# Scaling the weights of the later projections two pairs ahead, with the first scalings tied to the program's order

## The chip, the core and the metric

The kernel runs on one core of a Trainium2 chip. A core has five engines that work side by side, each through its own instructions in order: TensorE (PE in the profile, its weight loads PEld), VectorE (DVE), ScalarE (ACT), GpSimd (POOL) and SyncE (SP), which here only issues DMA transfers. They meet through semaphores. The metric is the device time of one execution in microseconds (us); less is better. All data is float32.

## The reference

Two layers work on x of shape 4 x 512 x 128 x 64 (batch b, time t, and f x h, together d = 8192). The part that matters is the beginning of layer 0:

```
xn = layernorm(x.reshape(b, t, d), ln_attn_g, ln_attn_b)
k = xn @ Wk
v = xn @ Wv
r = sigmoid(xn @ Wr)          # Wk, Wv, Wr: 8192 x 64
s_t = decay * s_(t-1) + k_t * v_t     # scan over time
x = x + (r * states) @ Wo
```

After it layer 0 has a convolution over frequency (with a norm and a gelu), a depthwise convolution over time (with two norms) and a feed-forward block from 64 to 256 and back. Layer 1 takes a moving average over time, filters the rest in the Fourier domain with 128 modes, and adds both.

## The kernel before

The 8192 features lie on partitions in 64 chunks of 128. Nearly all loops of layer 0 run over 32 *pairs* of chunks (`NPR`), with the 512 times along the free axis. For each batch there are these stages, written as generators:

- `project` (J): k, v, r and one more product, summed in PSUM over all pairs,
- `scan` (Z): the norm applied afterwards to the summed products, and the scan over time,
- `attend_and_convolve` (A), `convolve_time` (C), `open_feed` (O) and `feed_forward` (F).

The first norm is not applied to x. Its scale `ln_attn_g` is multiplied into the weights, and its mean and variance are applied in `scan`. So `project` loads, for each pair, the weights and the transposed x (`load_x`, line 295), multiplies the weights by the scale (`scale_weights`, line 358: two VectorE instructions of 128 x 192 for a pair, one for each chunk j), and multiplies (line 409: two products of 128 x 512 for each chunk in the program, each of which is two in the trace). Besides, x is loaded a second time with time on partitions (line 333), and VectorE takes its statistics (`statistics`, line 341).

For batches 2 and 3, which this text calls the later projections (`b > 1`), the weights come two pairs at a time (`weights`, line 351, 512 KB, issued on SP at every even pair for the two pairs after next). They lie in a ring of two buffers (`wx`). The scan uses the same ring for its own scratch (lines 474 to 487), and for b of 2 and 3 `feed_forward` uses it for line 758. Activations (`xp`) have a ring of three.

**Order.** TensorE's order is the program's own (`manual_schedule`). `in_turn` takes two stages of different batches at a time and draws from the two generators by fixed shares. Batch 2 is projected while batch 0 is in its feed-forward block, batch 3 while batch 1 is. At the end of each projection its scan runs between the last steps of the same feed-forward block. At its beginning the ends of `attend_and_convolve` and `convolve_time` are in TensorE's order: `finish` (line 264 sums, line 269 copies) and `moments` (lines 275 to 278, with a power of -1/2 on GpSimd, lines 233 and 234).

The orders of VectorE, ScalarE, GpSimd and SP are made by a planner when the program is built: it sets instructions by their readiness in its own model, and an instruction whose inputs it takes to be early may move far ahead of its place in the program. `tc.keep_in_program_order(i)` forbids that in one respect: i stays behind the instruction that the program wrote just before it for the same engine. It is no wait. If that earlier instruction has itself been moved ahead, i may move ahead with it.

In the feed-forward block, which runs beside the later projections, `widen` multiplies (line 732), ScalarE applies the gelu (line 737), `narrow` multiplies back (line 745) and ends with line 758 on VectorE, and `store` transposes its result on TensorE (line 764). VectorE also makes the next inputs there (lines 691, 692, 703) and, in the projections' first parts, time convolutions for the next batch (lines 613, 616, 625).

In the scan, line 470 multiplies k and v into place, lines 474 to 489 end in the state, lines 483 to 491 in `rst`, which line 496 multiplies.

## Time and profile before

| what | value |
| --- | --- |
| median of 3 runs | 3748.59 us |
| the runs | 3748.67, 3748.59, 3736.15 us |
| profiled execution | 3734.79 us |
| its span, first to last instruction | 3733.0 us |
| mean granted TensorE clock | 0.981 |
| TensorE busy | 3521.2 us, 94% |
| VectorE busy | 2671.9 us, 72% |
| ScalarE busy | 1778.0 us, 48% |
| later projections | about 795 to 1140 us and 1465 to 1806 us |
| their scans | about 1140 to 1200 us and 1806 to 1870 us |

In the profile's lines a group is named by line, engine, operation and output <- input, with the numbers of buffers left out. In a timeline a line holds the start, the duration, the instruction and how many of it follow each other; a bracket gives the idle time of the engine before it and what ended that. `DMA` in a bracket is a transfer, `issue` is time in which the engine waited for nothing that the profile shows.

### The profile page before, as it was taken

To read this page: it belongs to the slowest core of one execution; us is meant where nothing else is said; L and a number is where in the kernel's file an instruction comes from. 1 tells how busy PE (TensorE), PEld (TensorE's weight loads), DVE (VectorE), ACT (ScalarE), POOL (GpSimd) and SP (SyncE) were. 2 spreads that over 40 slices of the span, in tenths; PEclk is the share of its full clock that TensorE was granted. 3 is DMA by queue.
4 is the path that set the end of the run, shared out by engine and by line. 5 is a ranking of instruction groups with operands and counts; after the bars stand their busy time and mean duration, and the time that the engine had idled before them with its cause. 6 is when DMAs were issued, how large, how long until landed. Compare 5 with 4: busy or idle time off the path is not lost. (4 is left out here: it accounts for less than half of the span.)

```text
span 3733.0 us, 53000 instructions
## 1 busy us (share of the span) xinstructions
PE 3521.2 (94%) x20041; PEld 1360.6 (36%) x20041; DVE 2671.9 (72%) x3498; ACT 1778.0 (48%) x2331; POOL 447.3 (12%) x654
## 2 busy tenths in 40 slices
PE   9999999999998999999989989999989999989998
PEld 4433322234333223433322233333323843328533
DVE  4455569976776896676789699946658277792677
ACT  0012346655656565565656578868854200152100
POOL 0000012210101221001122122100000000001000
PEclk9999999999999999999999999999999999999999
DMA  9867657787874687788578677645569478894687
GB/s 314 279 211 242 227 177 262 260 276 265 290 262 168 235 280 271 266 292 278 182 238 286 213 247 267 234 149 196 198 203 287 150 240 290 290 297 164 213 294 260
DMA packets 427223, 910.29 MB, mean 244 GB/s; under 512 B 32728, under 2 KB 83160, under 8 KB 422872
## 3 DMA queue, kind: packets, MB, share of 16 engines
q1 hardware_dynamic: 353136, 636.92, 52.5%
q0 software_dynamic: 71680, 268.46, 19.7%
q8 instruction: 160, 2.62, 0.3%
q10 hardware_dynamic: 2152, 1.51, 0.1%
q14 instruction: 95, 0.78, 0.1%
HBM read 638.26 MB, written 268.50 MB: 243 GB/s over the span
## 5 line engine op out<-in xcount | busy, mean ns | idle before, releaser
L745 PE MATMUL p<-mid,w_sb 64*64 64x512 f32 x2048 | 554.5, 599 | 20.3 <-DVE wx L758 20.3
L745 PE MATMUL pb<-mid,w_sb 64*64 64x512 f32 x2048 | 536.2, 598 | 0.0
L737 ACT ACTIVATE mid<-c,fb_sb 128x1024 f32<-128x1024 f32 x256 | 284.3, 1111 | 97.2 <-PE c L732 94.8
L737 ACT ACTIVATE mid<-m,fb_sb 128x1024 f32<-128x1024 f32 x256 | 284.6, 1112 | 93.5 <-PE m L732 92.1
L732 PE MATMUL c<-x,w_sb 64*64 64x512 f32 x2016 | 281.2, 611 | 13.2 <-ACT mid L737 6.9
L732 PE MATMUL m<-x,w_sb 64*64 64x512 f32 x2016 | 283.0, 612 | 6.7 <-ACT ob L777 4.9
L745 PEld LDWEIGHTS p<-mid,w_sb 64*64 64x64 f32 x2048 | 155.5, 135 | 294.9 <-issue 262.0
L409 PE MATMUL a<-xp,wx 128*128 128x512 f32 x512 | 242.6, 617 | 9.1 <-DVE wx L358 8.6
L1043 ACT COPY two<-a 128x512 f32<-128x512 f32 x64 | 37.5, 585 | 428.9 <-PE a L1038 428.9
L1066 PE MATMUL b<-xin,avg_sb 128*128 128x512 f32 x512 | 230.8, 593 | 3.3 <-DVE xin L1072 3.3
L1072 DVE TENSOR_TENSOR xin<-b,pm 128x512 f32<-128x512 f32 x256 | 159.1, 683 | 100.2 <-PE b L1069 85.3
L570 ACT ACTIVATE sq<-x 128x1024 f32<-128x1024 f32 x128 | 135.1, 1055 | 181.4 <-DVE x L567 181.3
L625 DVE SCALAR_TENSOR_TENSOR to<-kd,vec,to 128x510 f32<-128x510 f32 (+1 forms) x272 | 197.1, 744 | 9.8 <-ACT to L621 8.7
L700 ACT ACTIVATE kd<-kd,vec 128x512 f32<-128x512 f32 x256 | 192.8, 803 | 3.1 <-DVE kd L692 3.1
L252 PE MATMUL st<-x,ones 128*32 128x512 f32 x512 | 176.8, 603 | 13.1 <-DVE x L567 13.1
L925 DVE COPY xf<-b 128x256 f32<-128x256 f32 x128 | 54.4, 425 | 178.3 <-PE b L1012 169.4
L625 DVE SCALAR_TENSOR_TENSOR z<-x,vec,z 128x511 f32<-128x511 f32 x240 | 175.9, 745 | 5.3 <-ACT z L621 3.0
L531 DVE TENSOR_TENSOR x<-a,xp 128x1024 f32<-128x1024 f32 x128 | 156.1, 1220 | 30.6 <-PE a L529 28.4
L703 DVE TENSOR_TENSOR x<-kd,kx 128x1024 f32<-128x1024 f32 x126 | 154.1, 1223 | 32.8 <-ACT kd L700 32.7
L529 PE MATMUL a<-rst,wo_sb 64*128 64x512 f32 x512 | 147.0, 648 | 27.1 <-DVE x L531 25.1
L758 DVE SCALAR_TENSOR_TENSOR x4t<-p,fb_sb,x 128x512 f32<-128x512 f32 x64 | 47.9, 748 | 172.0 <-PE pb L745 169.6
L692 DVE TENSOR_TENSOR kd<-kd,rm 128x1024 f32<-128x1024 f32 x128 | 155.7, 1220 | 7.8 <-ACT rm L286 6.3
(269 smaller groups left out, 6755.1 us busy)
## 6 DMA issues: line engine op xcount, KB each, us to landing
xp<-in_xt SPq DMA_DIRECT2D x256, 512.0 KB
kh<-to SPq DMA_DIRECT2D x156, 512.0 KB
x<-x POOLq DMA_DIRECT2D x128, 512.0 KB, 4.6
kx<-x SPq DMA_DIRECT2D x128, 512.0 KB
x<-ob POOLq DMA_DIRECT2D x64, 1024.0 KB, 8.0
xin<-x SPq DMA_DIRECT2D x64, 1024.0 KB
out<-xin POOLq DMA_DIRECT2D x64, 1024.0 KB, 6.6
x<-x SPq DMA_DIRECT2D x96, 512.0 KB
```

What stands on the lines that cost most here:

```text
L252: nc.tensor.matmul(st[32 * q : 32 * q + 32, :], lhsT=ones, rhs=src[:, j, :], start=first, stop=last,)
L409: nc.tensor.matmul(pa[:, k, :], lhsT=wq[:, j, k * P : (k + 1) * P], rhs=xp[:, j, :], start=first and j == 0, stop=last and j == 1,)
L531: nc.vector.tensor_tensor(x1, at, xp, ALU.add)
L625: tap = nc.vector.scalar_tensor_tensor(to[:, j, k:], xr[:, j, : SL - k], vec[:, w, c], to[:, j, k:], ALU.mult, ALU.add)
L692: nc.vector.tensor_tensor(d, d, pair_of(mb), ALU.subtract)
L700: tc.keep_in_program_order(nc.scalar.activation(d[:, j, :], d[:, j, :], AF.Identity, bias=vec[:, B4, c], scale=vec[:, G4, c]))
L703: nc.vector.tensor_tensor(x3, d, x2, ALU.add)
L732: nc.tensor.matmul(pm[halves[j], h, :], lhsT=w1_sb[halves[h], q * H : (q + 1) * H], rhs=x3[halves[h], j, :], start=True, stop=True,)
L737: nc.scalar.activation(mid, pm, AF.Gelu_apprx_tanh, bias=fb1_sb[:, q : q + 1])
L745: nc.tensor.matmul(sums2[i][j][halves[h], :], lhsT=w2_sb[halves[j], q, :], rhs=mid[halves[j], h, :], start=q == 0, stop=q == 3,)
L1066: nc.tensor.matmul(po[j], lhsT=avg_sb[:, j, :], rhs=xin[:, j, :], start=True, stop=False)
L1072: nc.vector.tensor_tensor(by_n(xin[:, j, :]), by_n(po[j]), by_c(pm[j % 2][:, j // 2, :]), ALU.add)
```

## The change

In the later projections:

- the scalings of the first *two* pairs are written ahead of the loop, and both are tied to the program's order (before: the first pair's only, and not tied),
- in the loop the scaling of pair i + 2 is written behind the products of pair i, where before the scaling of pair i + 1 was written ahead of the products of pair i. All of them are tied, as before.

Batches 0 and 1 are as they were, and so is the number of instructions.

```diff
         if b > 1:
             weights(0)
-            scale_weights(0, ws[0])
+            for k in range(2):
+                scale_weights(k, ws[k], True)
             xps[0] = load_x(b, 0)
...
             if b < 2:
                 scale_weights(i, wq)
-            elif not last:
-                scale_weights(i + 1, ws[i + 1], True)
             for j in range(2):
                 for k in range(2):
                     nc.tensor.matmul(
                         pa[:, k, :], lhsT=wq[:, j, k * P : (k + 1) * P], rhs=xp[:, j, :],
                         start=first and j == 0, stop=last and j == 1,
                     )
+                if b > 1 and j == 1 and i + 2 < NPR:
+                    scale_weights(i + 2, ws[i + 2], True)
                 yield 1.0
```

In the built program TensorE's order is the same before and after. VectorE's changes as follows. Before, the six scalings of the first three half buffers (pairs 0 to 2) stand in the scan of the batch before, some 300 instructions ahead of their products; after, they stand behind line 278 of the moments that the program writes just before the projection. In the loop the two scalings of a slot stand ahead of its two statistics instead of behind them, and in parts of the projection a scaling stands one slot earlier. On SP two loads change places with a neighbour, one in each later projection.

## The prediction

> **What bounds the kernel now.** I read the page's head first, then the chain that ended last, the waits of TensorE, and the timelines of TensorE and VectorE at every wait that has to do with line 358. The head:

> ```profile
> span 3733.0 us, 53000 instructions
> PE 3521.2 (94%) x20041; PEld 1360.6 (36%) x20041; DVE 2671.9 (72%) x3498; ACT 1778.0 (48%) x2331; POOL 447.3 (12%) x654
> L409 PE MATMUL a<-xp,wx 128*128 128x512 f32 x512 | 242.6, 617 | 9.1 <-DVE wx L358 8.6
> ```

> TensorE is the bound, busy for 94%, and its order is written out by hand. A time is gained or lost only where TensorE stands still or runs at half clock. Its waits, with total, count and longest:

> ```profile
> PE c L764 <- DVE x4t L758: 15.9, 9, 4.7
> PE a L409 <- DVE wx L358: 8.6, 2, 4.3
> PE m L764 <- DVE x4t L758: 8.1, 7, 4.3
> ```

> The second line is the scaling itself coming late, once in each later projection. TensorE's timeline, then VectorE's, around the first:

> ```profile
> 1054.95 3.78 PE L409 MATMUL a<-xp,wx 128*128 128x512 f32 x4 [4.29 <-DVE wx L358]
> ```

> ```profile
> 1052.26 1.22 DVE L616 TENSOR_TENSOR x<-x,rm 128x1024 f32<-128x1024 f32 x1
> 1053.39 1.28 DVE L341 BATCH_NORM_STATS2 stt<-x 128x6 f32<-128x512 f32 x2
> 1054.59 0.53 DVE L358 TENSOR_SCALAR wx<-wx,vec 128x192 f32<-128x192 f32 x2
> ```

> Here two pairs' products follow each other without a feed-forward block between them. The second pair's scaling stands behind VectorE work that took until 1054.6. The same wait, also 4.29 us, ends at 1720.83 in the last projection. The 4.3 and 4.7 us of line 764 are less plain. They lie in the scan of batch 2, at 1150 to 1178; VectorE first:

> ```profile
> 1156.41 0.55 DVE L358 TENSOR_SCALAR wx<-wx,vec 128x192 f32<-128x192 f32 x2 [3.31 <-DMA wx<-in_wkvr]
> 1156.87 0.75 DVE L758 SCALAR_TENSOR_TENSOR x4t<-p,fb_sb,x 128x512 f32<-128x512 f32 x1
> ...
> 1174.15 0.55 DVE L358 TENSOR_SCALAR wx<-wx,vec 128x192 f32<-128x192 f32 x2 [3.42 <-DMA wx<-in_wkvr]
> 1174.61 0.74 DVE L758 SCALAR_TENSOR_TENSOR x4t<-p,fb_sb,x 128x512 f32<-128x512 f32 x1
> ```

> ```profile
> 1157.77 1.09 PE L764 MATMUL m<-ident,x4t 128*128 128x128 f32 x4 [4.30 <-DVE x4t L758]
> ...
> 1175.50 1.09 PE L764 MATMUL c<-ident,x4t 128*128 128x128 f32 x4 [4.71 <-DVE x4t L758]
> ...
> 1184.29 0.64 PE L496 MATMUL a<-rst,qo 64*64 64x512 f32 x1
> ```

> These scalings belong to batch 3, whose products start at 1465. The planner has floated them 300 us ahead, where VectorE stops for weights just asked for (issues at 1146.15 and 1170.75) and line 758 stands behind it.

> [...]line 758 had its input and waited behind line 358. [...]after the 4.29 us wait four products took 3.57 us from start to start of the next, against 1.77 us (half of 3.53 for eight at 1078.79), and the eight transposes of line 764 took 1.71 instead of 0.97. [...]here the load issued at 1170.75 freed VectorE at 1174.15, 3.4 us, and the one at 1146.15 only at 1156.41, 10.3 us.

> **The change part by part.** Nothing is added or removed: each scaling is still two VectorE instructions of about 0.31 us, the DMAs are the same, and in the built changed kernel TensorE's order is the same to the instruction. Only VectorE's order moves, with two swaps on SP and one or two on ScalarE and GpSimd.

> (a) *Scaling one slot earlier.* In the built order scaling now stands ahead of the statistics (line 341) in each slot, and in the stretch up to the wait at 1055 one whole slot earlier. The pair that TensorE waited for is then scaled in the slot of 1035, TensorE arrives at 1050.7, and its activations (issued 1039.57) are there. The gain is the wait and the half clock behind it: 4.29 + (3.57 - 1.77) + (1.71 - 0.97) = 6.8 us. In the last projection it is 4.29 + 1.80 + (1.57 - 0.97) = 6.7 us. Sum 13.5.

> (b) *First scalings tied.* They leave both scans. For the scan of batch 2 the trace holds its own control: the scan of batch 3 has no projection behind it, so no line 358 stands in it, and its VectorE order is the one that the changed kernel has in batch 2's.

> ```profile
> 1833.62 0.63 PE L764 MATMUL c<-ident,x4t 128*128 128x128 f32 x4 [2.31 <-DVE x4t L758]
> ...
> 1840.90 0.64 PE L496 MATMUL a<-rst,qo 64*64 64x512 f32 x1 [0.77 <-DVE rst L491]
> ```

> From the first product of line 470 to that of line 496 it takes 1840.90 - 1816.20 = 24.7 us; batch 2 takes 1184.29 - 1150.46 = 33.8. The gain is 9.1 us, less than the waits, because a shorter wait for line 758 stays and rst is late next. In the scan of batch 1 (462 to 479) six scalings cost VectorE 1.9 us while TensorE waits for none of them: 0, at most 0.6.

> (c) *What the tie costs.* The first scaling of a projection is now behind line 278, the end of the moments before it, which waits for GpSimd's root.

> ```profile
> 794.52 0.17 DVE L269 COPY me<-a 128x8 f32<-128x8 f32 x1 [3.15 <-PE a L264]
> ...
> 798.33 0.16 DVE L278 TENSOR_TENSOR mrs<-me,rs 128x4 f32<-128x4 f32 x1 [1.19 <-POOL rs L234]
> ```

> ```profile
> 794.75 1.55 PE L409 MATMUL a<-xp,wx 128*128 128x512 f32 x3 [0.26 <-DVE me L269]
> ```

> Until now the products start at 794.75. They will start at 798.33 + 0.1 + 0.31 + 0.06 = 798.8: 4.05 us. In the last projection line 278 stands at 1467.06 and the products at 1465.24: by the same steps 2.3 us. TensorE has nothing else in its order there. Half clock after these gaps: 0 to 2.5 us each by the case at 1055; I take 2 for the first and 1 for the second, which already starts slow now (twelve products in 7.1 us). Sum 9.4, bounds 6.4 to 11.4. The statistics and the second moments (line 269 at 808.52) queue behind these scalings and one on the load issued at 804.30. That load moves with the products of pair 1 and by 3.4 us lands about as line 269's products end: 0, but up to 7 if it takes 10.3.

> (d) *Scaling nearer to its load.* In most slots the load was issued 8.5 to 16 us ahead; in two slots of each projection about 6 (issue 953.00, new slot 959). At 3.4 us this is free; at 10.3 us VectorE would stop for 4 us, of which its idle wait for the sums of line 745 (4.9 us in every other block) hides most. I take 0, bounds 0 to 4. The statistics come 0.5 us later and have until the projection's end. On SP one load of x and one of weights change places with a neighbour; each is wanted over 6 us later: 0.

> Sum: -13.5 - 9.1 + 9.4 = -13.2 us. The bounds are -22.6 - 0.6 + 6.4 = -17 on one side and, with 11.4 + 7 + 4, about 0 on the other. If in (c) products catch up with a later wait that they meet anyway, up to 6 us more is gained.

> The profiled execution took 3734.79 us, span 3733.0, so the sum makes 3721.6. The runs lie on two levels, 3748.67 and 3748.59 above, 3736.15 and the profiled one below; the median is the upper one. From the upper the sum gives 3735.4, from the lower about 3722. I take the lower level as likelier for a median of new runs and, since it may be mixed, **3725 us**.

> **Rivals.** *More than I count* (3735.5 - 24 = 3711): no half clock at the starts, and every later wait on VectorE shortened by the slack. For it speaks that DVE is busy for 242 of 346 us in a projection and full at 1050 to 1060; against it that elsewhere in the projection TensorE waits for almost nothing.

> *Gain given back* (about 3744, no change): the second moments wait for the late load, and half clock follows both starts, 9.4 + 2 + 7 = 18.4 against 22.6. For it the load of 10.3 us; against it that this one came behind other issues in a burst.

> *Weights late in every even pair, ending slower* (3770 and more): VectorE stops at the scaling for weights issued in the same pair, and line 758 behind it stalls TensorE. The place is the projection's slots, some 14 loads in each of two projections. To lie over 0.5% above 3748.6 it must eat 13.2 + 18.7 = 32 us, 1.1 us a load. With slots at 8.5 us and more behind the issue and 4.9 us of idle time behind them, it decides from a landing of about 14 us on. Only one load in the profile came near that, so I hold it unlikely.

> *That the change doesn't do what it says* can be excluded for the order, which is fixed when built, not for the cost.

> **How the numbers follow.** Forecast mechanism 0.68, more 0.12, given back 0.10, slower 0.10. A run-to-run step of 0.5% (18.7 us) is about what can be told from no change. Within the forecast mechanism the lower level, or a sum near its favourable end, lies under 3729.9 and counts as faster (0.43 of the 0.68), the rest as no change. With "more" that makes 0.55 faster; 0.25 + 0.10 makes 0.35 same; slower 0.10. The forecast mechanism by itself spans 3716 to 3740; with "more" on one side and most of "given back" on the other the range is 3708 to 3750.

> **What would show it.** The waits of line 409 for line 358 at 1055 and 1720 are gone, and new ones of about 4 and 2.3 us stand before the first product of each later projection. Line 764 waits in batch 2's scan for about 1 and 2.3 us instead of 4.3 and 4.7, and the stretch from line 470 to 496 takes 24.7 us. I am wrong if line 358 shows idle time for its DMA in many slots, if line 269 of the second moments is held up at a start, or if a new wait of line 764 appears within the projections.

## The result

The changed kernel takes 3727.17 us (median of 9 runs, 3719.89 to 3740.68), the kernel before beside it 3737.15 us (9 runs, 3726.41 to 3748.67). The ratio is 0.9968, 95% interval 0.9953 to 0.9982: faster by about a third of a per cent. That is small, but the interval leaves out 1, and so do those of two more measurements of the same two kernels, 0.9968 (0.9952 to 0.9983) and 0.9980 (0.9965 to 0.9995). The profiled execution took 3727.17 us.

In the changed kernel's profile the products are line 408 (before: 409), and the lines behind the loop are 1 higher than before (470 is 471, 496 is 497, 758 is 759, 764 is 765). Lines up to 358 are the same. The head of the profile after, and the products' group:

```profile
span 3725.4 us, 53006 instructions
PE 3519.4 (94%) x20041; PEld 1366.8 (37%) x20041; DVE 2671.6 (72%) x3498; ACT 1779.8 (48%) x2331; POOL 450.4 (12%) x654
L408 PE MATMUL a<-xp,wx 128*128 128x512 f32 x512 | 240.0, 613 | 6.6 <-issue 6.6
```

TensorE's waits, with total, count and longest:

```profile
PE c L765 <- DVE x4t L759: 12.9, 8, 2.3
PE a L408 <- issue: 6.6, 2, 4.1
...
PE m L765 <- DVE x4t L759: 4.1, 6, 0.9
```

No wait of the products for the later weights of line 358 (`wx`) is left; before it was 8.6 us in two. The waits of the transposes for line 759 are 3.0 and 4.0 us shorter. In their place stand two new waits of the products, 4.05 and 2.58 us. TensorE's timeline names no releaser for them:

```profile
802.96 3.75 PE L408 MATMUL a<-xp,wx 128*128 128x512 f32 x4 [4.05 <-issue]
...
1461.23 3.75 PE L408 MATMUL a<-xp,wx 128*128 128x512 f32 x4 [2.58 <-issue]
```

VectorE's timeline at the first of them does: the eight instructions of pairs 0 to 3 stand right behind line 278, which waits for GpSimd. (Pairs 2 and 3 are written behind the products of pairs 0 and 1, but nothing else of VectorE's stands between, so they follow at once.)

```profile
802.46 0.16 DVE L278 TENSOR_TENSOR mrs<-me,rs 128x4 f32<-128x4 f32 x1 [2.43 <-POOL rs L234]
802.54 1.92 DVE L358 TENSOR_SCALAR wx<-wx,vec 128x192 f32<-128x192 f32 x8
804.38 1.28 DVE L341 BATCH_NORM_STATS2 stt<-x 128x6 f32<-128x512 f32 x2
```

The scan of batch 2 after the change, on TensorE and then on VectorE:

```profile
1153.87 1.12 PE L471 MATMUL a<-kvrg,sel 128*128 128x512 f32 x2
1157.82 1.22 PE L765 MATMUL m<-ident,x4t 128*128 128x128 f32 x8 [0.95 <-DVE x4t L759]
...
1171.29 1.22 PE L765 MATMUL c<-ident,x4t 128*128 128x128 f32 x8 [2.31 <-DVE x4t L759]
1178.57 0.64 PE L497 MATMUL a<-rst,qo 64*64 64x512 f32 x1 [0.82 <-DVE rst L492]
```

```profile
1156.92 0.75 DVE L759 SCALAR_TENSOR_TENSOR x4t<-p,fb_sb,x 128x512 f32<-128x512 f32 x1 [0.42 <-PE pb L746]
...
1170.42 0.72 DVE L759 SCALAR_TENSOR_TENSOR x4t<-p,fb_sb,x 128x512 f32<-128x512 f32 x1
```

Line 358 has gone from it, line 759 follows its sums, and from line 471 to line 497 it takes 1178.57 - 1153.87 = 24.7 us instead of 33.8.

**Place by place.** All kernels below run the same 20041 products on TensorE in the same order. So the start of the n-th product in one profile less its start in the profile of before is a running account, and its growth over a place is what the place gained or lost. In us, times of the places by the profile of before:

| kernel | start of projection 2 (786 to 806) | wait at 1055 | scan of batch 2 (1140 to 1200) | start of projection 3 (1455 to 1490) | wait at 1720 | sum | all else |
| --- | --- | --- | --- | --- | --- | --- | --- |
| changed | +5.0 | -6.6 | -9.1 | +2.9 | -6.5 | -14.3 | +6.7 |
| changed, second | +5.0 | -6.6 | -9.1 | +2.3 | -6.5 | -14.9 | +10.0 |
| changed, third | +4.3 | -6.6 | -9.1 | +3.7 | -6.5 | -14.2 | -0.5 |
| tie only | +6.3 | +0.1 | -7.1 | +3.1 | 0.0 | +2.4 | -3.4 |
| loop only | -1.6 | -6.6 | +1.2 | +0.2 | -6.5 | -13.3 | +9.5 |
| two ahead, before the products | +6.3 | -6.6 | -7.0 | +3.6 | -6.5 | -10.2 | +5.8 |
| one ahead, behind the products | +5.0 | -0.9 | -9.2 | +4.6 | -0.8 | -1.2 | +111.0 |
| early tie | +2.9 | -6.6 | -9.1 | +1.0 | -6.5 | -18.3 | +7.7 |
| earlier tie | -0.6 | -6.6 | -9.1 | 0.0 | -6.5 | -22.8 | +0.9 |
| earlier tie, second | -2.3 | -6.6 | -9.1 | -1.0 | -6.5 | -25.5 | +15.4 |

The five places repeat to a microsecond or two. The last column doesn't, and most of it is probably where half-clock stretches fall, of which the last section tells (in the one-ahead kernel it holds new waits too). A single profiled time is therefore no test of a change this small; the places are, and medians of many runs.

### The profile page after: what moved, and what is told of

Its sections match the earlier page's. It is cut to its first block, busy times and chain, and to the rows that moved or that the text cites. A ratio compares the mean times of both kernels' runs of the same rounds, so it can differ in the third digit from the quotient of the medians.

```text
span 3725.4 us, 53006 instructions
## 1 busy us (share of the span) xinstructions
PE 3519.4 (94%) x20041; PEld 1366.8 (37%) x20041; DVE 2671.6 (72%) x3498; ACT 1779.8 (48%) x2331; POOL 450.4 (12%) x654
## 5 line engine op out<-in xcount | busy, mean ns | idle before, releaser
L704 DVE TENSOR_TENSOR x<-kd,kx 128x1024 f32<-128x1024 f32 x126 | 154.2, 1224 | 33.8 <-ACT kd L701 33.8
L569 POOL DMA_DIRECT2D x<-x x128 | 93.5, 731 | 566.7 <-DVE x L568 561.7
```

The source lines that it names most:

```text
L704: nc.vector.tensor_tensor(x3, d, x2, ALU.add)
```

## The experiments

My theory going in: the gain is two waits (13 us) and one scan (9 us), less two starts (8 us). The rivals: only one half of the change does anything; the half clock behind the waits is chance; the starts' cost is absorbed.

### The tie alone

```
-            scale_weights(0, ws[0])
+            for k in range(2):
+                scale_weights(k, ws[k], True)
...
-            elif not last:
+            elif 0 < i < NPR - 1:
                 scale_weights(i + 1, ws[i + 1], True)
```

> The kernel before with only the tie: pairs 0 and 1 are scaled in the program's order ahead of slot 0, and from slot 1 on each slot scales the next pair ahead of its own products, as before. My theory (four places, each counted for itself): the scan of batch 2 gains its 9.1 us (line 497 one full clock stretch earlier after line 471), the two starts cost 4.05 + 1 and 2.3 + 0.6, together 7.9 us, and the two waits of 4.29 us of the projection's products for line 358, at about 1055 and 1720 us, stay. Sum -1.2 us, ratio 0.9997. Rival (all of the gain is the loop's, the scan's stall is covered by the other stream): +8 us, ratio 1.002. Rival (the tie's cost at the start is absorbed later): -9 us, ratio 0.9976.

Measured: 3744.95 us against 3741.44, ratio 1.0006 (0.9993 to 1.0019). The waits of this kernel (410 is the line of the products):

```profile
PE a L410 <- DVE wx L358: 8.6, 2, 4.3
...
PE a L410 <- issue: 6.6, 2, 4.0
```

Both of before's waits stay, both new ones are there, and the scan's place gains 7.1: from its first product of line 471 to line 497 it takes 25.2 us instead of 33.8, and a half-clock stretch just ahead of that takes 1.6 us back. No gain of the tie by itself can be told: what it takes out of the scan it puts at the starts. Both rivals (1.002 and 0.9976) lie outside the interval, the first only just.

### The loop's move alone

```
             for k in range(2):
-                scale_weights(k, ws[k], True)
+                scale_weights(k, ws[k], k > 0)
```

(against the changed kernel; pair 0 may float ahead again, and pair 1 with it)

> The kernel before with only the loop's move: pair i + 2 is scaled behind pair i's products, pair 0 is not tied and pair 1 is tied to pair 0 alone, so both still run in the scan of the batch before. My theory: the two waits of 4.29 us for line 358 at about 1055 and 1720 us go (with the half clock behind them 6.6 and 6.5 us), the scan of batch 2 keeps its two waits for the weights' load, and the starts of the two projections cost nothing. Sum -13.1 us, ratio 0.9965; the scan now holds seven or eight scalings in place of six, 0.3 us each, which may take up to 1 us back. Rival (the scan's tie is where the gain comes from): 0 to -4 us, ratio 0.999 to 1.000. Rival (the gain is chance of where half-clock stretches fall): between -5 and +5 us, with the waits at 1055 and 1720 gone all the same.

Measured: 3730.96 us, ratio 0.9969 (0.9960 to 0.9979), the same as the whole change on the same chip (0.9968). Its waits:

```profile
PE c L765 <- DVE x4t L759: 15.4, 9, 4.2
...
PE m L765 <- DVE x4t L759: 8.6, 7, 4.4
```

They are those of before (15.9 and 8.1): the scan still stops for the weights' load. The two waits for line 358 are gone, and the starts cost nothing. So the net gain of the change is the loop's, and 13.3 us at its five places agrees with the 13.1 expected. Both rivals (0.999 and above, or within 5 us of the kernel before) lie outside the interval.

### Distance or place in the slot

The loop's edit changes two things, how many pairs ahead and whether ahead of the products or behind them. First the new distance at the old place:

```
             if b < 2:
                 scale_weights(i, wq)
+            elif i + 2 < NPR:
+                scale_weights(i + 2, ws[i + 2], True)
...
-                if b > 1 and j == 1 and i + 2 < NPR:
-                    scale_weights(i + 2, ws[i + 2], True)
```

> The changed kernel with pair i + 2 scaled ahead of pair i's products in place of behind them; the tie of the first two stays. It asks whether the distance of two pairs or the place in the slot took the waits for line 358 away. My theory (the distance): no wait of the products for line 358 at about 1055 and 1720 us, ratio 0.9968, at most 0.9975 since VectorE may wait a little for loads issued in the same slot. Rival (the place behind the products, which gives the load time): VectorE waits for the load in each even slot and holds the statistics and the other stream's work up, waits for line 358 come back, ratio 0.999 or above.

Measured: 3725.59 us, ratio 0.9970 (0.9960 to 0.9980), no wait for the later weights of line 358. The place in the slot is not needed for the gain. Then the old distance at the new place:

```
-                if b > 1 and j == 1 and i + 2 < NPR:
-                    scale_weights(i + 2, ws[i + 2], True)
+                if b > 1 and j == 1 and 0 < i < NPR - 1:
+                    scale_weights(i + 1, ws[i + 1], True)
```

> The changed kernel with the distance of one pair left and only the place changed: pair i + 1 is scaled behind pair i's products; the tie of the first two stays. My theory (the distance is what counts): the two waits for line 358 at about 1055 and 1720 us are there again, 4.3 us or more each, and with the half clock behind them the gain of 13 us is lost: ratio 0.9968 + 0.0035 = 1.000. Rival (the place): both waits stay away, ratio 0.9968.

Measured: 3828.84 us, ratio 1.0243 (1.0220 to 1.0266). The direction was mine, the size was not: I had counted on before's two waits, and there are seventeen.

```profile
PE a L408 <- DVE wx L358: 76.8, 17, 4.8
```

VectorE's timeline at one of them shows why:

```profile
897.32 0.75 DVE L759 SCALAR_TENSOR_TENSOR x4t<-p,fb_sb,x 128x512 f32<-128x512 f32 x1 [6.18 <-PE pb L746]
897.98 0.74 DVE L759 SCALAR_TENSOR_TENSOR x4t<-pb,fb_sb,x 128x512 f32<-128x512 f32 x1
899.08 1.22 DVE L704 TENSOR_TENSOR x<-kd,kx 128x1024 f32<-128x1024 f32 x1 [0.36 <-ACT kd L701]
900.23 1.22 DVE L614 TENSOR_TENSOR x<-x,rm 128x1024 f32<-128x1024 f32 x1
901.36 1.22 DVE L692 TENSOR_TENSOR kd<-kh,rm 128x1024 f32<-128x1024 f32 x1
902.50 1.22 DVE L617 TENSOR_TENSOR x<-x,rm 128x1024 f32<-128x1024 f32 x1
903.63 0.54 DVE L358 TENSOR_SCALAR wx<-wx,vec 128x192 f32<-128x192 f32 x2
```

VectorE sat for 6.18 us on the feed-forward block's sums, then spent another 6.3 us on that block's line 759, its next inputs and two instructions of the time convolution, and only then came to two instructions of a third of a microsecond that TensorE had been standing for since 899.2. The same group, with the statistics behind it, stood ahead of the late scaling at 1055 in the kernel before. It began with

```profile
1047.08 0.75 DVE L758 SCALAR_TENSOR_TENSOR x4t<-p,fb_sb,x 128x512 f32<-128x512 f32 x1 [4.95 <-PE pb L745]
```

There, too, scalings stood behind such groups, but only in two slots was TensorE there first. In the changed kernel the pair that had come late is scaled ahead of the group, and its products, the last four of these twelve, start at 1060.48 without a wait, 15 us behind their scaling:

```profile
1045.21 0.54 DVE L358 TENSOR_SCALAR wx<-wx,vec 128x192 f32<-128x192 f32 x2
```

```profile
1056.95 5.42 PE L408 MATMUL a<-xp,wx 128*128 128x512 f32 x12
```

This is the mechanism of the loop's gain: not VectorE's speed, but which group of the other stream's instructions, with a wait at its head, a scaling stands behind. Nor is it the load: in the run one pair ahead, behind the products, the profile shows no idle time of VectorE in front of line 358 in the later projections. The distance decides between waits and none. The place in the slot matters as well where the lead is only one pair: two waits ahead of the products, seventeen behind them. The profiled execution is 3844.57 - 3727.17 = 117 us longer than the changed kernel's; 76.8 of that are the waits. The rest, 40 us, is not settled one by one; the half-clock time grew from 132 to 270 us, part of it inside the waits.

### The tie's cost taken away

If the starts' cost comes from standing behind line 278, an earlier tie must recover it. The first version scales pairs 0 and 1 between lines 276 and 278, while VectorE waits for GpSimd: `between` is `begin_next`, which runs the next projection, from its first load of weights, up to the scaling of its first two pairs (the scaling is line 355 there, the products line 412):

```
         nc.vector.tensor_tensor(var, square, var, ALU.subtract)
+        if between:
+            between()
         rsqrt(rs, var)
...
+        def begin_next():
+            begun[b + 1] = project(b + 1)
+            next(begun[b + 1])
```

> The changed kernel, but the first two pairs' scaling is tied one step earlier: behind the subtraction that makes the variance of the moments, ahead of the product that waits for GpSimd's inverse root, so that eight scalings of 0.24 us stand in VectorE's idle time of 2.4 us there. My theory: the four gains of the changed kernel stay, and the two starts cost nothing: the first product of each later projection waits no longer for a scaling. That is 7.9 us less than the changed kernel, ratio to the kernel before 0.9968 - 0.0021 = 0.9947. Rival (the first product waits at the starts for something else too, its input or the stream ahead of it, or the gap passes on to the next product that waits for the moments): within 2 us of the changed kernel, ratio 0.9965. Rival (the scaling delays the moments' last product and what waits for it): slower than the changed kernel by 1 to 4 us, ratio 0.997 to 0.998.

Measured: 3724.24 us, ratio 0.9954 (0.9937 to 0.9971); the changed kernel beside it 3729.93 (0.9968). The two ratios can't be told apart with these few runs, the places can: the starts lost 2.9 and 1.0 instead of 5.0 and 2.3, about half. VectorE's timeline at the first start (four scalings belong to the two pairs, not the eight that I had expected):

```profile
797.91 0.17 DVE L269 COPY me<-a 128x8 f32<-128x8 f32 x1 [3.00 <-PE a L264]
...
798.84 0.16 DVE L276 TENSOR_TENSOR var<-me,var 128x4 f32<-128x4 f32 x1
798.92 1.14 DVE L355 TENSOR_SCALAR wx<-wx,vec 128x192 f32<-128x192 f32 x4
```

The scaling still stands behind the copy of line 269, which waits for TensorE itself, and so the products start 1.46 us late. I had overlooked that the chain begins there. The second version puts the same call at the head of `finish`, ahead of that copy:

```
     def finish(st, bank, tag, ahead=None):
 
+        if ahead:
+            ahead()
         s_sb = rowp.tile([P, SL], F32, tag="s", name="s_sb")
```

> As the early tie, one step earlier still: pairs 0 and 1 are scaled ahead of the copy that takes the sums of the moments out of PSUM, where VectorE is idle 3.0 us (first later projection) and 4.0 us (second). In the early tie the first products still waited 1.46 and 0.93 us, since the scaling stood behind the copy and the variance. My theory: these waits go down to the 0.3 us that the kernel before has there, and with the half clock behind them the two starts lose 2.9 and 0.5 us less. That is 3.4 us less than the early tie, ratio to the kernel before 0.9954 - 0.0009 = 0.9945, and about 8 us less than the changed kernel. Rival (what the waits give, other half-clock stretches take[...]): ratio 0.9954, with the waits gone all the same. Rival (four scalings ahead of the copy delay the moments and the bank that they free): a wait of the first product on line 271 of 1 us or more, ratio 0.996 or above.

Measured: 3717.63 us, ratio 0.9956 (0.9939 to 0.9973). TensorE's first products of the projection:

```profile
799.38 1.98 PE L412 MATMUL a<-xp,wx 128*128 128x512 f32 x4 [0.26 <-DVE me L271]
```

The wait is 0.26 us, as in the kernel before, with full clock behind it (four in 1.98 us; in the changed kernel 3.75). All five places hold their gain at once, -22.8 us. But the ratio had not moved from the first version's, as the first rival said, so I ran it against the changed kernel on one chip:

> The tie ahead of the copy of the moments' sums once more, beside the changed kernel on one chip: does it beat it? My theory: the two starts' 7.9 us are saved, so its median is 8 us below the changed kernel's and its ratio to the kernel before 0.9947 to 0.9956. In the profile, both first products wait 0.3 us. Rival (half-clock stretches that fall elsewhere take it back): within 3 us of the changed kernel.

> The changed kernel a third time, as the other side of that comparison: ratio to the kernel before 0.9968 within 0.0015, waits of 4.0 and 2.3 us ahead of the first products.

Measured: the earlier tie 3724.48 us (16 runs), ratio to before 0.9949 (0.9935 to 0.9963); the changed kernel 3733.97 (14 runs), 0.9980 (0.9965 to 0.9995). By the means of these runs, 3725.2 and 3733.8, one is 0.9977 of the other, 95% interval 0.9964 to 0.9991 by resampling them. It beats the kernel before, and the changed one by 9.5 us in the medians where 8 were expected.

### The changed kernel again

> The changed kernel once more, unchanged, beside the others: the measure of what two runs of one kernel differ by. My theory: a ratio of 0.9968 within 0.0015. In its profile the five places have the same waits as in the first one (4.05 and 2.3 us ahead of the first products, no wait for line 358), while the half-clock stretches that follow no wait of more than 2 us fall elsewhere. Rival (half-clock stretches are set by the kernel's own waits): the same stretches at the same times within 1 us.

Measured: 0.9968 (0.9952 to 0.9983). The waits at the five places are as in the first profile. Of the half-clock stretches some fall alike and some don't: two between 435 and 497 us in the first profile, one in the second, and the account over the first 786 us, which the change doesn't touch, differs by 3.3 us between two profiles of one kernel.

## Why the prediction was right, and where not

The mechanism held at every place, and the predicted time, 3725 us, is 2 us from the median.

(a) *Scaling one slot earlier*, 13.5 us: right. The places gave 6.6 + 6.5 = 13.1 in every kernel that scales two pairs ahead, nothing with the tie alone, and 0.9 and 0.8 with one pair ahead behind the products. "One slot earlier" is the right cause, and the two runs on distance and place add why a slot counts.

(b) *First scalings tied*, 9.1 us from the control in batch 3's scan: right to the tenth. Batch 2's scan takes 24.7 us now, and the waits that stay are 0.95 and 2.31 us, where about 1 and 2.3 were said. The scan of batch 1, put at 0, takes 16.76 us before and after.

(c) *What the tie costs*, 9.4 us: right in kind, a little high. From the last sum of line 264 to the first product it takes 4.30 and 2.83 us in place of 0.51 each, so the gaps cost 3.8 and 2.3, where 4.05 and 2.3 were said. The half clock behind them added 0.5 to 1.2 and 0 to 1.4 in three profiles, not 2 and 1; part of it the kernel before had at these starts too (its granted clock from 786 to 806 us is 0.91, the changed kernel's 0.77; from 1455 to 1490 us 0.95 and 0.90). Sum 7.9 (5.0 + 2.9) in the first profile. That the second moments would not be late was right, but it was close: line 269 runs at 818.74, as TensorE's sums end (818.70), and the scaling of pair 4 ahead of it ended only at 818.59.

```profile
818.04 0.55 DVE L358 TENSOR_SCALAR wx<-wx,vec 128x192 f32<-128x192 f32 x2 [12.39 <-PE a L408]
```

The profile names the products. They hold the buffer until pair 1's end; then the load of pairs 4 and 5 into it was issued, at 814.51. The scaling started 3.5 us behind that, so most likely the load was what it waited for last. The prediction had reckoned with 3.4 us; with 10.3 the second moments would have been late.

(d) *Scaling nearer to its load*, 0: right. In the later projections VectorE is idle in front of line 358 only twice, 12.4 us at the place just named and 1.4 us at 1475, and TensorE doesn't wait for either.

The sum was -13.2; the places give -14.3, the three medians -10.0, -11.5 and -9.9. The difference is not explained place by place; -14.3 lies inside the first measurement's interval, which is -17.6 to -6.7 us.

What failed is the step from the sum to a chance. I read three runs of before as two levels, took 3748.6 as the median and let a median on the lower level count as faster by over 0.5%, with 0.55. In 35 runs of the kernel before on one chip the times lie between 3724 and 3753 us, half of them between 3735.8 and 3745.5, median 3741.4, and between 3731.8 and 3749.3 no gap is wider than 2.1 us. There are no two levels, the median of three was at the upper end of a scatter, and 13 us on it are 0.35%. The likely outcome was "no change" within 0.5%, which I had at 0.35. That the predicted time is so near is partly owed to this: -13.2 from the true middle of about 3740 makes 3727.

Of the rivals, *more than I count* put the change at -24; its places gave -14.3. Only the earlier tie, which takes the starts' loss away, comes near it, with -22.8 and -25.5 at the places. *Gain given back* and *weights late in every even pair* didn't happen. But the run one pair ahead, behind the products, shows that a loss of the size I put at 3770 and more was near: it takes 103 us more than the run two pairs ahead on the same chip (3828.84 against 3725.59), by VectorE's order and not by the load.

## What to carry to other kernels

A short instruction that the bounding engine needs should be placed by what stands ahead of it in its engine's queue, not by its own inputs; one step more of lead is worth having where that queue holds another stream's group with a wait in it (here two instructions of 0.31 us, behind such a group, held TensorE for 4.29 us twice, and with one pair of lead behind the products for up to 4.8 us seventeen times). When a tie keeps an instruction from floating too far, look at what it is now tied behind: here the nearest place in the program lay behind a chain through three engines (lines 264, 269, 234 and 278), which cost 4.05 and 2.58 us at the starts, and the same tie put ahead of that chain kept the gain without the price. For a change of a third of a per cent, compare the account at each place, and many runs; one profile's total can hide it.

## What the runs showed that I had not expected

```
idle in the step, us      next step at half clock
0   to 0.7                   11 of 10515
0.7 to 1.1                   21 of   411
1.1 to 1.5                   18 of   197
1.5 to 2.0                   63 of   171
2.0 to 2.5                  109 of   109
2.5 to 3.4                   85 of    85
```

In the profiles before and after the change alone the last two lines are 18 of 18 and 13 of 13. The ends of products are modelled, so the borders are not sharp, and what lies behind the steps was not shown. In these traces, then, what followed a pause went with how the pause fell in the steps. Behind the scan of batch 3 (at 1884 us in the kernel before) a pause of 2.65 us from product to product is the same in all eleven profiles to 0.01 us, and so is one of 1.4 us behind it in all but one (1.1). In eight of them a half-clock stretch of 3.4 to 10.2 us follows and costs 1.4 to 4.5 us; there one step holds 2.0 us of idle time or more. In three (before, the tie alone, one pair ahead behind the products) the pause began 1.7 to 1.8 us into a step and was shared out between two, at most 1.7 us to a step, and no half clock follows. Where the steps lie against the kernel differs between two executions of one kernel: the pause began at 2.38, 0.20 and 2.63 us of a step in the three profiles of the changed one. That is most of the column "all else" of the table as far as I can tell, and it fits the scatter of 3724 to 3753 us: over those 35 runs the time falls as the mean granted clock rises (0.974 to 0.984, correlation -0.74). That it is all of either was not tested.
